# A hybrid block on one core: the inverse's levels on the full array, the scan's output products in one run, and a new instruction order

## The chip, the cores and the metric

The kernel runs on one core of one Trainium2 chip. The metric is the device time of one launch in microseconds (us). A core has a matrix engine (PE in the profile, TensorE here; its weight loads are listed apart as PEld), a vector engine (DVE), an activation engine (ACT), a general engine (POOL) and SP, which here only issues transfers. Each engine executes its instructions in the order in which they stand in the program, and engines wait for each other by semaphores. TensorE reads operands from the on-chip memory SBUF and writes results to PSUM, which has eight banks of 128 partitions x 512 float32.

## The reference, cut to what matters

32 sequences of 256 tokens with 128 features go through four residual stages:

```
x = x + attn_a(layernorm(x))      # gated delta rule
x = x + ffn(layernorm(x))         # silu(x Wg) * (x Wu), then Wd; hidden 384
x = x + attn_b(layernorm(x))      # convolution + state-space scan + gate
x = x + ffn(layernorm(x))
```

`attn_a` is a recurrence over tokens with a state S of 128 x 128 for each sequence:

```
S = S @ (a_t * (I - b_t * k_t k_t^T)) + b_t * v_t k_t^T ;  o_t = (q_t @ S) * g_t
```

Taken in chunks of 128 tokens, it becomes products of matrices and the inverse of a unit triangular 128 x 128 matrix for each chunk (the identity plus the decayed, beta-weighted products of keys). `attn_b` projects to z, x, B, C and dt, applies a causal convolution of four taps and silu to x, B and C, and computes for each of four heads `(C B^T * L) (x dt)` with `L[i, j] = exp(sum of dA from j+1 to i)`, adds a skip and what earlier tokens' state carries over, gates with silu(z), normalizes and projects. Everything is float32.

## The kernel before, in words

**Tiling.** Two sequences make a unit (`SEQS = 2`), so there are 16 units; a unit is NT = 4 tiles of 128 tokens, and most of its tiles are 128 partitions x 512 columns. A unit's work is four stages that follow one another: `attention` (stage 0, names ending in `_a`), `ffn` (stage 1, `_f`), `ssd` (stage 2, `_s`) and `ffn` again (stage 3, `_h`). Units don't depend on each other.

**Order.** No engine's order is the order of the source. `Planner` collects every operation of all 16 units with its engine, an assumed duration and an assumed latency, then `run` (L306) plays a list schedule: at each step it takes, over all engines, the operation that can start first, and among those of one engine that could start within 20 ns the one with the smallest key. The key (L316) is `at(unit)`, which is the unit's number times `period` (15,000 ns), plus how far from the end of its unit's longest chain the operation lies, plus an offset of its stage (`STAGE`). For the last three units `at` packs the starts closer (`LAST`). At most five units beside the oldest may be in work (`window`), a buffer must be free (`SLOTS`), a PSUM bank is given out only `EARLY` ns ahead of the work that fills it, and a change of ACT's function table counts as `SWITCH` ns in the key. The instructions are emitted in the order of the planned start times, and this is the program's order on each engine. Nothing in it adapts on the chip: an instruction whose operand is late holds what stands behind it on its engine.

**Helpers and lines.** All operations go through helpers, so the profile shows their lines: L214 `matmul`, L224 `transpose` (a product with the identity), L232 and L234 `act` (a copy, a function), L248 `vec`, L265 `pool`, L275 `dma` (issued by SP). A float32 product is executed as two passes, each with a weight load and a matmul record, so the counts in the profile are twice those of the source; a transpose is one pass. A form such as `128*64 128x64` is a pass whose weights take 128 rows and 64 columns of the array and that streams 64 columns.

**The inverse** (`attention`, L760 to L827). The 16 x 16 diagonal blocks of `diag` (the negated strictly triangular part of a chunk) go through DRAM: eight transfers write them to `blocks`, and eight more, one for each group of 16 partitions, broadcast them to `rows_n`. DVE inverts the blocks in 15 steps (`step`, `u`), and POOL spreads the result to the block diagonal of `x`. Then the blocks are doubled three times (`LEVELS = (16, 32, 64)`). A level transposes x (four passes), copies the result to SBUF (ACT, `t`), multiplies with `diag` (eight passes, `p1`), copies (ACT, `pm`), multiplies with x (eight passes, `p3`) and writes the off-diagonal blocks into x. Levels 16 and 32 stream all 128 columns of each tile, and DVE writes with a mask (COPY_PREDICATED, 128x512). Level 64 has a single off-diagonal block, and its operands are quarter tiles: 64 rows and 64 columns of the array, 64 columns streamed, three ACT copies of 64x256. In the profile p1 and p3 are `p_a<-t_a,neg_a` and `p_a<-x_a,pm_a`.

**The scan's output** (`ssd`, L1001 to L1024). For each sequence and each of its two tiles c, a product in bfloat16 makes the exponents (`pl`), ACT takes the exponential, DVE multiplies with the masked `cb` (`sm`), and then eight products (four heads, two halves of the tokens) write `sy_ps`. Each uses 128 rows and 64 columns of the array; the two halves stand beside each other in it. The eight products of a tile are operations of their own for the planner.

**The log-decay sums** (`ssd`, L928 to L936). `grid` holds 32 columns; a product with the triangle `le` sums them over tokens (`cs`). Its weights use 32 columns of the array.

What is touched beside this: the masks of the levels (L495 to L504, set up once) and the constants of the planner (L150 to L160).

Of the kernel before, what the change touches and what calls it, by code (L numbers as in the profile page):

```python
# [145 lines left out]
class Planner:  # L146
# [5 lines left out]
    SWITCH = 60000.0  # L152
    HOP, SLACK = 50.0, 0.0
    STAGE = (-100.0, -1400.0, -2700.0, -4400.0)
    EARLY = 2800.0
    SPARE = {"ps": 0.5, "m": 3, "l": 0.5, "t": 1, "s": 2, "d": 0.5, "g": 0.5, "b": 0.5, "e": 0.5}
    LAST = 0.26
    HALF = "be"
    RATE = 270.0
    LANES = 8  # L160
    SIZES = {"ps": 512, "m": 512, "l": 1024, "t": 64, "s": 32, "d": 512, "g": 8192, "b": 384, "e": 12288}
# [16 lines left out]

    def add(self, eng, busy, late, emit, outs, ins, table=None, after=(), lock=False):
# [4 lines left out]
        op.moves = 0.0  # L184
# [24 lines left out]
    def matmul(self, out, lhsT, rhs, start, stop, passes=2, cost=None):  # L209
# [10 lines left out]
        self.add("PE", busy, 165, emit, [out], [lhsT, rhs], after=after)  # L220

    def transpose(self, out, in_, ident, cost=109):
        def emit():
            self.tc.nc.tensor.transpose(real(out), real(in_), real(ident))  # L224

        self.add("PE", cost, 165, emit, [out], [in_, ident])
# [74 lines left out]
    def at(self, unit):  # L301

        late = max(0, unit - (self.units - 3))
        return (unit - late + late * self.LAST) * self.period

    def run(self):  # L306
# [20 lines left out]
        moved, landed = 0.0, []  # L327
        cands = {e: [] for e in engines}
# [6 lines left out]
        while len(order) < len(ops):  # L335
            best = None
            for e in engines:
                rest = []
                for op in cands[e]:
# [24 lines left out]
                if e == "ACT" and table is not None:  # L364
# [3 lines left out]
                    ]  # L368
                pick = min(same, key=lambda x: x[0])
# [4 lines left out]
            if op.eng == "ACT" and op.table and table not in op.table:  # L374
                t += 1300
                table = op.table[0]
                self.loads += 1
            for b in op.bufs:
# [49 lines left out]
def hybrid_block(ctx: ExitStack, tc: tile.TileContext, ins: dict, out: bass.AP):  # L428
# [35 lines left out]
    pl = Planner(tc, pools, period=15000.0, window=5)  # L464
# [31 lines left out]
    for d in LEVELS[:-1]:  # L496
        nb = P // (2 * d)
        m = pl.const([P, P], f"m_{d}")
        pool("memset", m, 0.0)
        v = m.rearrange("p (b h e) -> p b h e", h=2, e=d)[:, :, 1, :]  # L500
        pool("memset", v, 1.0)
        select(v, ALU.is_ge, 0, [[-2 * d, nb], [0, d]], 1)
        select(v, ALU.is_ge, d - 1, [[2 * d, nb], [0, d]], -1)
        mask_x.append(m.bitcast(I32)[:, None, :].to_broadcast([P, NT, P]))  # L504
# [20 lines left out]
    select(least, ALU.is_ge, 2 * (parts + 5), [[1, P]], -2)  # L525
    for i in range(2):
        sums_s.append(pl.const([P, NT, P], f"sums_s{i}", BF16, again=True))
# [120 lines left out]
    def attention(g, x):  # L648
# [120 lines left out]
        for b in range(NBLK):  # L769
            at = slice(b * BLOCK, (b + 1) * BLOCK)  # L770
            size = NT * BLOCK * BLOCK
            pl.dma(
                spread.part(at),
                blocks[0, b * size : (b + 1) * size].via(lambda ap: ap.partition_broadcast(BLOCK)),
                late=2100,
            )
# [19 lines left out]
        for lv, d in enumerate(LEVELS[:-1]):  # L796
            pt = bank([P, NT, P], f"pt_{n}_{d}")
            for j in range(NT):
                pl.transpose(pt[:, j, :], xi_f[:, j, :], ident)
            t = big([P, NT, P], f"t_{n}_{d}")  # L800
            copy(t, pt)
            p1 = bank([P, NT, P], f"p1_{n}_{d}")
            for j in range(NT):
                matmul(p1[:, j, :], diag[:, j, :], t[:, j, :], True, True)
            pm = big([P, NT, P], f"pm_{n}_{d}")
            copy(pm, p1)
            p3 = bank([P, NT, P], f"p3_{n}_{d}")
            for j in range(NT):
                matmul(p3[:, j, :], pm[:, j, :], xi_f[:, j, :], True, True)
            vec("copy_predicated", xi_f, mask_x[lv], p3, ins=(xi_f,), more=17)  # L810

        d = LEVELS[-1]
        lo, hi = slice(0, d), slice(d, P)
        pt = bank([P, NT, d], f"pt_{n}_{d}").part(lo)
        for j in range(NT):
# [293 lines left out]
```

## Time and profile before

| | us |
|---|---|
| median of 3 runs | 880.75 (879.32 to 882.31) |
| the profiled execution: device time | 885.61 |
| its span, from the first to the last instruction | 882.9 |
| TensorE busy (matmul records) | 842.9, 95% of the span |
| DVE / ACT / POOL busy | 687.5 / 608.1 / 351.9 |
| level-64 products and transposes (64*64 forms) | 12.9 + 11.2 + 6.6 |
| output products of the scan (128*64 form) | 41.9 |
| mean granted TensorE clock | 0.986 of full |

A row of a timeline is a run of equal instructions on one engine: its start, how long it lasts to the end of its last record, and their number. Matmul records overlap, since the ends of pipelined passes are modelled; what a run really takes from TensorE is the time from its start to the start of the next row. On TensorE with its work back to back the row of 128x128 passes advances by some 0.11 us a pass, and one of 512 streamed columns by some 0.43 us.

### The profile page before, as it was taken

What the parts mean: (1) busy time and instruction counts of PE and PEld (TensorE: products, weight loads), DVE (VectorE), ACT (ScalarE), POOL (GpSimd) and SP (SyncE); (2) the same over time, 40 slices, a digit from 0 to 9 for tenths busy, and PEclk for the clock granted to TensorE, in tenths of its full rate; (3) what the DMA queues carried; (4) which work ended last, traced back from release to release, by engine and by line L of the source; (5) the groups of instructions that cost most, each with busy time, mean ns of one, the idle gap of its engine ahead of it and who ended that gap; (6) DMA issues with size and microseconds to landing.
All of it is one profiled execution on the core that took longest, in us unless ns stands there. A gap on an engine that the chain in (4) does not pass through costs nothing.

```text
span 882.9 us, 16763 instructions
## 1 busy us (share of the span) xinstructions
PE 842.9 (95%) x5625; PEld 622.3 (70%) x5625; DVE 687.5 (78%) x2314; ACT 608.1 (69%) x1393; POOL 351.9 (40%) x559
## 2 busy tenths in 40 slices
PE   5879999999999999999999999999999999999798
PEld 3557776676858678685867868587675886765675
DVE  4695879877796878878887888877988467679963
ACT  5744477467685967677686767869477477579762
POOL 7974213151626335071633607155062231322550
PEclk9979999999999999999999999999999999999899
DMA  5211011000111101011110101111101000000001
GB/s 144 72 49 47 11 28 28 4 26 4 38 30 37 28 15 48 7 37 30 37 28 15 47 8 37 29 38 39 30 25 30 14 13 4 2 13 13 11 2 36
DMA packets 42149, 25.39 MB, mean 29 GB/s; under 512 B 18448, under 2 KB 37840, under 8 KB 42064
## 3 DMA queue, kind: packets, MB, share of 16 engines
q1 hardware_dynamic: 40768, 24.00, 10.2%
q8 instruction: 44, 0.72, 0.3%
q10 hardware_dynamic: 1296, 0.33, 0.2%
q14 instruction: 41, 0.34, 0.1%
HBM read 19.16 MB, written 5.14 MB: 28 GB/s over the span
## 4 chain that ended last, share of the span: by engine, by line
PE 67%; DVE 17%; ACT 10%; issue 2%; DMA 2%; POOL 1%; SPq 1%; DVEq 0%; POOLq 0%; ACTq 0%
PE p_a L214 8%; PE pc_s L214 5%; PE fu_h L214 5%; PE fg_h L214 5%; PE fy_f L214 4%; PE fu_f L214 4%; PE fg_f L214 4%; PE fy_h L214 3%; PE so_s L214 2%; DVE sm_s L248 2%; ACT L234 2%; PE kk_a L214 2%; PE wq_a L214 2%; DVE e_a L248 2%; PE sy_ps_s L214 2%
## 5 line engine op out<-in xcount | busy, mean ns | idle before, releaser
L248 DVE SCALAR_TENSOR_TENSOR cy_s<-pc_s,cw,cy_s 128x510 f32<-128x510 f32 (+2 forms) x192 | 137.0, 735 | 3.8 <-ACT cy_s L234 3.4
L234 ACT ACT_TABLE_LOAD x64 | 82.1, 1283 | 10.9 <-DMA bk<-in_L_attn_a_bk_dram 8.4
L214 PE MATMUL fy_f<-wdT,hT_f 128*128 128x128 f32 x384 | 75.7, 282 | 0.4 <-DVE hT_f L248 0.4
L214 PEld LDWEIGHTS fy_f<-wdT,hT_f 128*128 128x128 f32 x384 | 61.3, 191 | 15.7 <-issue 10.5
L214 PE MATMUL fy_h<-wdT,hT_h 128*128 128x128 f32 x384 | 71.7, 280 | 0.0
L214 PEld LDWEIGHTS fy_h<-wdT,hT_h 128*128 128x128 f32 x384 | 58.1, 191 | 10.2 <-issue 8.6
L214 PE MATMUL pc_s<-xT_s,w_xbc 128*128 128x512 f32 x128 | 62.3, 596 | 0.4 <-ACT zs_s L234 0.4
L265 POOL TENSOR_SCALAR ab_a<-ab_a 128x8 f32<-128x8 f32 x16 | 3.6, 227 | 147.1 <-ACT ab_a L234 147.0
L248 DVE TENSOR_TENSOR step_a<-rows_a,u_a 128x28 f32<-128x28 f32 (+14 forms) x240 | 53.3, 225 | 10.9 <-DMA rows_a<-blocks_a 5.6
L265 POOL TENSOR_TENSOR x_a<-u_a,blk 128x512 f32<-128x512 f32 x16 | 21.0, 1315 | 87.3 <-ACT qT_a L234 27.4
L234 ACT ACTIVATE cy_s<-pc_s,cb,cw 128x512 f32<-128x512 f32 x64 | 49.1, 780 | 8.3 <-PE pc_s L214 7.2
L248 DVE TENSOR_TENSOR u_a<-u_a,step_a 128x28 f32<-128x28 f32 (+14 forms) x240 | 50.2, 213 | 5.1
L214 PE MATMUL p_a<-x_a,pm_a 128*128 128x128 f32 (+1 forms) x384 | 52.7, 263 | 0.0
L214 PEld LDWEIGHTS p_a<-x_a,pm_a 128*128 128x128 f32 (+1 forms) x384 | 44.1, 173 | 11.9 <-issue 6.1
L234 ACT ACTIVATE fth_h<-fg_h 128x512 f32<-128x512 f32 x48 | 28.6, 597 | 34.3 <-PE fg_h L214 33.7
L214 PE MATMUL fu_f<-xT_f,wuT 128*128 128x512 f32 x96 | 49.8, 617 | 0.9 <-ACT fth_f L234 0.9
L214 PE MATMUL fu_h<-xT_h,wuT 128*128 128x512 f32 x96 | 50.1, 606 | 0.0
L214 PEld LDWEIGHTS p_a<-t_a,neg_a 128*128 128x128 f32 (+1 forms) x384 | 43.2, 178 | 9.7 <-ACT t_a L232 3.3
L214 PE MATMUL fg_h<-xT_h,wgT 128*128 128x512 f32 x96 | 49.2, 600 | 0.0
L214 PE MATMUL p_a<-t_a,neg_a 128*128 128x128 f32 (+1 forms) x384 | 48.5, 266 | 0.6 <-ACT t_a L232 0.5
L234 ACT ACTIVATE xn_s<-x,shift_s,rstd_s 128x128 f32<-128x128 f32 x64 | 26.4, 486 | 31.3 <-DVE shift_s L248 31.2
L265 POOL TENSOR_TENSOR xd_s<-xt_s,dt_s 128x512 f32<-128x512 f32 x32 | 32.8, 1043 | 37.1 <-ACT xt_s L232 37.1
(211 smaller groups left out, 2400.9 us busy)
## 6 DMA issues: line engine op xcount, KB each, us to landing
rows_a<-blocks_a SPq DMA_DIRECT2D x128, 64.0 KB
x<-in_L_attn_a_x_dram SPq DMA_DIRECT2D x16, 256.0 KB
dec_a<-row_a SPq DMA_DIRECT2D x16, 256.0 KB
out_dram<-x SPq DMA_DIRECT2D x16, 256.0 KB
blocks_a<-neg_a SPq DMA_DIRECT2D x128, 4.0 KB
cuts_s<-cut_s SPq DMA_DIRECT2D x48, 8.0 KB
sums_t<-cuts_s SPq DMA_DIRECT2D x32, 12.0 KB
sums_s<-cuts_s SPq DMA_DIRECT2D x16, 24.0 KB
```

The costliest lines, as they stand in the source:

```text
L214: self.tc.nc.tensor.matmul(real(out), lhsT=real(lhsT), rhs=real(rhs), start=start, stop=stop)
L234: self.tc.nc.scalar.activation(real(out), real(in_), func, bias=real(bias), scale=real(scale), **kw)
L248: getattr(self.tc.nc.vector, name)(real(out), *map(real, args), **{k: real(v) for k, v in kw.items()})
L265: getattr(self.tc.nc.gpsimd, name)(real(out), *map(real, args), **{k: real(v) for k, v in kw.items()})
```

## The change

Level 64 is written like the other two. In all three levels, `t` keeps the copied half of each pair of blocks in its second half and receives the first product in its first half, and the two products stream only the columns of the half that is needed (64 of 128 for each tile), with weights of 128 rows and 128 columns. The two ACT copies of a level and the masked DVE write take 256 columns in place of 512; level 64 has a masked DVE write where it had an ACT copy. The buffer `pm` is gone. The masks are set up with 64 columns, for three levels.

The eight `rows` transfers become one, which names the broadcast in its source. The 32 columns of `grid` become part of a 128-column constant tile that is otherwise zero (two of them, for even and odd units), so that the product uses 128 weight columns; only 32 rows of its result are read. The sixteen output products of a sequence are one batch: the first waits for all that any of them needs, and the planner puts nothing else on TensorE between them.

The planner also counts 150 ns (`CUT`) when TensorE changes between products of at most 64 weight columns and wider ones, and adds 2,000 ns (`KEEP`) to the key of an operation that would make it change. Its constants are others: `period` is 30,000, the stage offsets are (0, -8600, 1900, 0), `LAST` is 0.13, `EARLY` 1400, and `SHIFT` moves single units. With them the order on every engine is planned anew.

```diff
-    SWITCH = 60000.0
-    HOP, SLACK = 50.0, 0.0
-    STAGE = (-100.0, -1400.0, -2700.0, -4400.0)
-    EARLY = 2800.0
+    SWITCH = 64000.0
+    HOP, SLACK = 50.0, 30.0
+    STAGE = (0.0, -8600.0, 1900.0, 0.0)
+    EARLY = 1400.0
-    LAST = 0.26
+    LAST = 0.13
+    SHIFT = (0.0, -3200.0, 0.0, 0.0, 1500.0, 6600.0, 1600.0, 0.0, 0.0, 0.0, 0.0, 0.0, 0.0, 0.0, -7000.0, -5400.0)
+    CUT = 150.0
+    KEEP = 2000.0
+    def batch(self, ops):
+        for op in ops[1:]:
+            for p in op.preds.values():
+                if p not in ops and p.n not in ops[0].preds:
+                    ops[0].preds[p.n] = p
+                    p.succs.append(ops[0])
+        for op in ops:
+            op.batch = ops
...
+        op.cut = 0 if cols > P // 2 else 1
...
-        return (unit - late + late * self.LAST) * self.period
+        return (unit - late + late * self.LAST) * self.period + self.SHIFT[unit]
...
-                for op in cands[e]:
+                for op in cands[e] if e != "PE" or not rest_of else rest_of:
...
+                if e == "PE":
+                    same = [((k[0] + (self.KEEP if op.cut != cut else 0), k[1]), t, op) for k, t, op in same]
...
+            if op.eng == "PE":
+                t += self.CUT if op.cut != cut else 0.0
+                cut = op.cut
+                rest_of = [o for o in op.batch if not o.placed and o is not op]
...
-    pl = Planner(tc, pools, period=15000.0, window=5)
+    pl = Planner(tc, pools, period=30000.0, window=5)
...
-        for b in range(NBLK):
-            at = slice(b * BLOCK, (b + 1) * BLOCK)
-            size = NT * BLOCK * BLOCK
-            pl.dma(
-                spread.part(at),
-                blocks[0, b * size : (b + 1) * size].via(lambda ap: ap.partition_broadcast(BLOCK)),
-                late=2100,
-            )
+        pl.dma(
+            spread,
+            blocks.via(
+                lambda ap: ap[0, :].rearrange("(b n) -> b n", b=NBLK)[:, None, :].to_broadcast(
+                    [NBLK, BLOCK, NT * BLOCK * BLOCK]
+                )
+            ),
+            late=2100,
+        )
...
-        for lv, d in enumerate(LEVELS[:-1]):
+        for lv, d in enumerate(LEVELS):
+            nb = P // (2 * d)
+            halves = xi_f.rearrange("p t (b h e) -> p t b h e", h=2, e=d)
             pt = bank([P, NT, P], f"pt_{n}_{d}")
             for j in range(NT):
                 pl.transpose(pt[:, j, :], xi_f[:, j, :], ident)
             t = big([P, NT, P], f"t_{n}_{d}")
-            copy(t, pt)
-            p1 = bank([P, NT, P], f"p1_{n}_{d}")
+            t_halves = t.rearrange("p t (b h e) -> p t b h e", h=2, e=d)
+            copy(t_halves[:, :, :, 1, :], pt.rearrange("p t (b h e) -> p t b h e", h=2, e=d)[:, :, :, 0, :])
+            p1 = bank([P, NT, nb, d], f"p1_{n}_{d}")
             for j in range(NT):
-                matmul(p1[:, j, :], diag[:, j, :], t[:, j, :], True, True)
-            pm = big([P, NT, P], f"pm_{n}_{d}")
-            copy(pm, p1)
-            p3 = bank([P, NT, P], f"p3_{n}_{d}")
+                matmul(p1[:, j, :, :], diag[:, j, :], t_halves[:, j, :, 1, :], True, True)
+            copy(t_halves[:, :, :, 0, :], p1)
+            p3 = bank([P, NT, nb, d], f"p3_{n}_{d}")
             for j in range(NT):
-                matmul(p3[:, j, :], pm[:, j, :], xi_f[:, j, :], True, True)
-            vec("copy_predicated", xi_f, mask_x[lv], p3, ins=(xi_f,), more=17)
-        d = LEVELS[-1]
...
+                matmul(p3[:, j, :, :], t[:, j, :], halves[:, j, :, 1, :], True, True)
+            vec("copy_predicated", halves[:, :, :, 1, :], mask_x[lv], p3, ins=(xi_f,), more=17)
...
-        grid = small_([P, 2, NH, NT], f"grid_{n}")
+        few = slice(0, 2 * NH * NT)
+        grid = grids[g % 2][:, few].rearrange("p (o h j) -> p o h j", o=2, h=NH)
...
-        pc = bank([P, P], f"cs_{n}").part(few)
-        matmul(pc, grid.rearrange("p o h j -> p (o h j)"), le, True, True)
+        pc = bank([P, P], f"cs_{n}")
+        matmul(pc, grids[g % 2], le, True, True)
+        pc = pc.part(few)
...
+            ms = []
             for c in range(2):
...
-                for h in range(NH):
-                    for to in (slice(0, P // 2), slice(P // 2, P)):
-                        matmul(
-                            py[:, c, h * HD : (h + 1) * HD].part(to), m[:, h, to], xd[:, c, h, :], True, True,
-                        )
+                ms.append(m)
+            pl.batch([
+                matmul(
+                    py[:, c, h * HD : (h + 1) * HD].part(to), m[:, h, to], xd[:, c, h, :], True, True, cost=62,
+                )
+                for c, m in enumerate(ms) for h in range(NH) for to in (slice(0, P // 2), slice(P // 2, P))
+            ])
```

## The prediction

> **What bounds the kernel now.** I read the page first (busy shares, the slices), then TensorE's busy time by stretches, then TensorE's timeline row by row, then the waits. TensorE is the bound: it is the one engine that is nearly always busy, and ahead of slice 5 and around slice 38 it is not.
>
> ```profile
> PE 842.9 (95%) x5625; PEld 622.3 (70%) x5625; DVE 687.5 (78%) x2314; ACT 608.1 (69%) x1393; POOL 351.9 (40%) x559
> ...
> PE   5879999999999999999999999999999999999798
> ...
> PEclk9979999999999999999999999999999999999899
> ```
>
> The stretches (columns: start:end, length, busy us and number of records of TensorE, its weight loads, DVE, ACT and POOL, granted clock, DMA share and GB/s):
>
> ```profile
> 0.00:44.00 44.00, 30.44 (x139) 20.58 (x140) 25.24 (x106) 28.19 (x85) 37.75 (x85) 1.00 0.42 107
> 44.00:100.00 56.00, 48.76 (x291) 38.40 (x290) 43.09 (x155) 26.16 (x66) 28.23 (x41) 0.91 0.16 42
> 100.00:820.00 720.00, 709.69 (x4813) 524.82 (x4813) 578.10 (x1946) 517.82 (x1161) 261.94 (x400) 1.00 0.09 24
> 820.00:850.00 30.00, 25.18 (x243) 18.74 (x239) 26.25 (x69) 22.36 (x51) 18.50 (x27) 0.89 0.03 6
> 850.00:882.90 32.90, 28.79 (x152) 19.74 (x150) 14.80 (x41) 13.53 (x30) 5.53 (x10) 0.97 0.08 25
> ```
>
> In the long middle TensorE idles 10.3 us of 720. Start and tail idle 13.6 + 7.2 + 4.8 + 4.1 = 29.7 us, and in two of them the granted clock is down (0.91, 0.89), which costs about 0.09 x 56 + 0.11 x 30 = 8 us more. So an edit is worth what it changes of TensorE's own occupancy, plus what the new order makes of about 40 us of idle time and 8 us of clock. ACT (69%) and DVE (78%) get lighter for nothing unless TensorE waits for them.
>
> **Occupancy.** A pass's price is the start of the next row less its own start. Level 64 and the narrow products sit between wide ones (TensorE's timeline):
>
> ```profile
> 400.94 1.05 PE L214 MATMUL p_a<-t_a,neg_a 128*128 128x128 f32 x8
> 401.83 0.59 PE L214 MATMUL fg_f<-xT_f,wgT 128*128 128x512 f32 x1
> ...
> 417.38 0.38 PE L214 MATMUL fy_f<-wdT,hT_f 128*128 128x128 f32 x2
> 417.69 0.68 PE L214 MATMUL p_a<-t_a,neg_a 64*64 64x64 f32 x8
> 418.30 1.12 PE L214 MATMUL fu_h<-xT_h,wuT 128*128 128x512 f32 x2
> ```
>
> Eight full passes take 401.83 - 400.94 = 0.89 us, 0.11 each. Two `fy_f` passes ahead of the quarter tiles take 0.31, not 0.22: 0.09 us to enter. The eight quarter passes take 0.61. Over all start times in the trace the medians are: full pass 112 ns, transpose 109; quarter pass 58, quarter transpose 56, entering +93, leaving +90. There are 59 runs of quarter tiles, mostly four to a unit.
>
> ```profile
> 385.14 0.38 PE L214 MATMUL po_a<-pr_a,k_a 128*128 128x128 f32 x2
> 385.46 0.34 PE L214 MATMUL sy_ps_s<-xd_s,sm_s 128*64 128x64 f32 x4
> 385.72 0.49 PE L214 MATMUL po_a<-pr_a,k_a 128*128 128x128 f32 x2
> 386.14 1.03 PE L214 MATMUL sy_ps_s<-xd_s,sm_s 128*64 128x64 f32 x28
> ```
>
> The output products: two `po_a` passes take 0.32 (0.09 to enter), four narrow passes 0.26: 4 x 0.032 (the median over pairs) and 0.12 to leave. So a run costs 0.21 us beside its work. There are 50 such runs. `cs` (128*32) takes 133 ns a pass, 93 to enter and 69 to leave, once a unit.
>
> **What will a pass of 128 weight columns cost that streams 64?** No such row exists; the nearest is `pe`, with 128 weight columns and 8 streamed:
>
> ```profile
> 381.63 0.38 PE L214 MATMUL fy_h<-wdT,hT_h 128*128 128x128 f32 x2
> 381.85 0.29 PE L214 MATMUL pe_s<-dA_s,le 128*128 128x8 f32 x2
> 382.00 0.47 PE L214 MATMUL fy_h<-wdT,hT_h 128*128 128x128 f32 x2
> 382.36 0.41 PE L224 MATMUL pt_a<-ident,x_a 128*128 128x128 f32 x2
> ```
>
> Six passes take 0.73 us, as six full ones do (0.67) and a little more, though two of them stream almost nothing. What `pe` seems to save (0.15 to the next row) `fy_h` gives back (0.36 for two): the weight loads keep their step of 0.11. Two sections of the Trainium skill, page "TensorE: Matmul & The Clock Gate", part here. "Back-to-back issue gap" prices a matmul by its streamed columns alone, so half the columns would be about half the time; "LDWEIGHTS" prices a load by weight columns, 128 / 1.2 = 107 ns. By the first, taking the 58 ns of the quarter row, levels 16 and 32 (32 product passes a unit) would save 32 x 54 ns = 1.73 us, and level 64 would lose its transposes only; by the second nothing is saved and level 64 pays full passes. The row decides for the second: 112 ns. The ends are 58 and 112.
>
> **The sum on TensorE, 16 units.**
> - Level 64 on full weights: 16 passes x (112 - 58) + 4 transposes x (109 - 56) = 1.08 us a unit: +17.2.
> - Its 59 mode runs gone: 59 x 0.183 = -10.8.
> - Output products: at most two runs a unit, so 50 to 32: 18 x 0.213 = -3.8.
> - `cs` padded: 2 x (112 - 133) - 93 - 69 = -0.20 us a unit: -3.3.
> Together -0.7 us. At 58 ns a pass it would be another 16 x (1.73 + 0.86) = -41.
>
> **What other engines get.** An ACT copy of 128x512 takes 594 and 583 ns, one of 64x256 takes 364 to 367; a copy of 4x128 takes 249 and one of 128x128 287, so columns set it, and I take 0.365 for 128x256: 4 x 0.22 + 0.365 (the last copy moves to DVE) = -1.25 us a unit, 20 of 608. The masked write is 728 ns for 512 columns; the nearest half-sized DVE reads of PSUM take 413 to 421: 2 x -0.31 + 0.41 = -0.2 us a unit. Both lie behind TensorE's work for other units: 0. Without that cover a unit's inverse chain would be 1.5 us shorter in levels 16 and 32 and 1.1 longer in level 64, still near nothing. Masks and the zeroed grids change a few POOL memsets ahead of the first unit's inverse: 0. The second grid is free again two units later: 0. The batch makes a sequence's first eight output products wait for the second tile's exponential and mask (0.59 + 0.68 us); behind them on TensorE stand other units' products, which the plan puts ahead instead: 0, or 16 x 2 x 1.3 = 41 us if nothing stood ready.
>
> **The row transfer.** Seven of eight issues go, 0.46 us apart on SP. In place of them comes a wait: the one transfer needs all eight block writes, where the first row transfer could leave at once.
>
> ```profile
> 344.73 4.22 SPq L275 DMA_DIRECT2D blocks_a<-neg_a  x7
> 349.00 3.66 SPq L275 DMA_DIRECT2D rows_a<-blocks_a  x8
> ```
>
> Before: 3.7 us of issues and 2.15 until the last landed (the chain shows it at 88.30), 5.8 us. After: some 1.8 (SP's longest wait for `cuts`, a like pair), 0.4 to issue, 2.15, and the spread of 128 rows of 4 KB at about 0.24 us: 7 more on each of 16 engines, 1.7. Sum 6.1. Here a rule speaks against the change: "DMA: Bandwidth & Descriptors", section "Why a DMA increments its semaphore by 16 and not by 1", has a transfer use the largest number of engines up to 16 that divides the slowest dimension of both sides; the source's is now 8. Then 15 more rows on each of 8 engines: 3.6, sum 8.0. Loss +0.3 to +2.2 us a unit. Behind SP's wait stand input loads and sums for other units, whose consumers come later. DVE waited 5.6 us in all for these rows; TensorE has other units' work: 0, but up to 2 at the first unit.
>
> **The order.** This decides. Of the 40 us idle, some 14 stay (TensorE starts at 10.3 us, behind the first loads; 4 us lie behind its last pass). Of the other 26, plus 8 of clock, I take two fifths: -14. Doubling `period` lets older units finish first; the last three units' starts are now packed to 386.9, 390 and 392.4 us of key, which mixes their tails, where all three now wait for DVE's convolution around 820 to 832. Bounds: -30 (nearly all of it) to +26 (below).
>
> Span 882.9 - 0.7 - 14 = 868. The profiled execution took 885.61, 4.9 above the median; from span to median it is -2.15, so **866 us**.
>
> **The rivals.**
> - *Half the streamed columns is half the time.* -41 on TensorE, of which DVE and hand-offs would return a part (I take 40%): 866 - 25 = 841. The row of `pe` speaks against it. 5%.
> - *The edits cancel and the order is worth nothing.* The middle is at 98.6% already, and the start hangs on loads and POOL (37.75 busy of 44). 880, from 877 to 884. 12%.
> - *Slower: the inverse's hand-offs come uncovered.* A level hands over three times between TensorE and ACT or DVE, nine times a unit. Each is a copy (0.37) and TensorE's resumption (waits for ACT ahead of weight loads show 0.2 to 0.7), say 0.8 us. Today rows of `fy_f`, `fu_h` and `pvq` from other units stand between them. With keys 30 us apart, units are mixed less, and an in-order queue waits. Two bare hand-offs a unit are 16 x 2 x 0.8 = 26 us; with head and tail unimproved the kernel becomes slower from the first quarter of one on (0.25 x 0.8 x 16 = 3). Against it: the plan places other work wherever it expects a wait. About 893, from 884. 25%.
> - *The forecast*: 850 to 877, 58%.
>
> **Range and chances.** From 848 (7% below) to 893 (half of the slower case above, 13%). A difference of 0.3%, 2.6 us, is about what can be told. Faster: the forecast, the 5%, a quarter of the second rival: 0.66. Same 0.09, slower 0.25.
>
> **What would show it.** `p_a` rows of 128x64 that advance by 0.11 us a pass (0.06 would prove the first rival); no 64*64 and no 128*32 forms; `sy_ps` in 16 to 32 runs; ACT busy near 588; TensorE idle in the first 100 and last 63 us down from 29.7 to about 20. I am wrong if TensorE's waits for `t` or `p_a` in the middle grow beyond 10.3 us, or if start and tail stay as they are.

## The result, and the profile after

The changed kernel takes 935.45 us (934.11 to 936.46), beside 880.37 us of the kernel before in the same comparison: 1.0622 times as long, with a 95% interval of 1.0598 to 1.0647. The forecast was 866 us and its range ended at 893. The profiled execution took 934.78 us and its span is 933.1 us, 50.2 more than before.

From the page of the changed kernel (busy us and share of the span, the slices, the granted clock, and the chain that ended last by engine and by line):

```profile
PE 845.4 (91%) x5625; PEld 636.9 (68%) x5625; DVE 677.2 (73%) x2330; ACT 608.2 (65%) x1391; POOL 353.0 (38%) x562
...
PE   5588998999998899999999899898997898998788
...
PEclk9889999999999899999999999999998999989999
...
PE 50%; DVE 19%; ACT 12%; DMA 11%; POOL 3%; issue 2%; SPq 2%; ACTq 0%; DVEq 0%; POOLq 0%
DMA rows_a<-blocks_a 9%; PE p_a L227 5%; DVE cy_s L264 4%; PE fg_h L227 4%; PE fy_f L227 4%; PE fu_h L227 4%; ACT L250 3%; PE fy_h L227 3%; PE fg_f L227 3%; PE fu_f L227 3%; PE pz_s L227 2%; SPq L291 2%; PE pc_s L227 2%; PE so_s L227 2%; DVE x L264 2%
```

TensorE executes the same 5,625 passes and is busy for about as long. Its row of slices, solid before from slice 4 to 37, now has eights and a seven throughout. At the head of the chain's list stands a transfer, `rows_a<-blocks_a`, with 9% of the span: the one that replaced eight.

The same stretches as before (start:end, length, busy us and records of TensorE, weight loads, DVE, ACT and POOL, granted clock, DMA share, GB/s):

```profile
0.00:44.00 44.00, 24.13 (x106) 16.13 (x106) 25.46 (x91) 21.20 (x62) 39.74 (x86) 0.94 0.39 100
44.00:100.00 56.00, 49.00 (x284) 38.13 (x285) 40.67 (x168) 29.48 (x83) 26.77 (x43) 0.90 0.20 48
100.00:820.00 720.00, 675.82 (x4610) 516.99 (x4609) 534.17 (x1845) 480.69 (x1082) 251.58 (x381) 0.98 0.09 24
820.00:850.00 30.00, 25.84 (x94) 15.33 (x95) 17.89 (x61) 20.21 (x47) 4.40 (x9) 0.88 0.00 0
850.00:933.10 83.10, 70.57 (x535) 50.35 (x533) 58.99 (x168) 56.64 (x119) 30.54 (x44) 0.98 0.06 17
```

In the middle TensorE idles 720 - 675.82 = 44.2 us, where it idled 10.3, and the clock there is 0.98 where it was 1.00. By 820 us the changed kernel has done 5,000 passes (106 + 284 + 4610); before it had done 5,243. The edits' own price is not the reason. TensorE's timeline (start, length, count of a run):

```profile
343.12 1.06 PE L227 MATMUL p_a<-t_a,neg_a 128*128 128x64 f32 x8
344.01 0.61 PE L240 MATMUL pt_a<-ident,x_a 128*128 128x128 f32 x4
...
449.80 2.09 PE L227 MATMUL sy_ps_s<-xd_s,sm_s 128*64 128x64 f32 x64
451.81 0.38 PE L227 MATMUL fy_f<-wdT,hT_f 128*128 128x128 f32 x1
```

Eight passes of 128 weight columns and 64 streamed ones take 344.01 - 343.12 = 0.89 us, 0.11 each: the streamed half buys nothing, as forecast. The output products of two sequences have met in one run: 64 passes in 2.01 us, one change of tile form where there were several.

To see where the 50 us went I took, over the whole trace, the step from each pass's start to the next start, and split it: the form's usual step, what is added where the tile form changes, and the rest (waits, and passes at a lower clock). The split is rough: the second column takes in waits that happen to fall on a change of form. At the prices in the prediction the 20 narrow runs that are left would be some 4 us.

| us | usual steps | form changes | the rest |
|---|---|---|---|
| before | 769.4 | 30.6 | 68 |
| after | 785.0 | 11.5 | 122.5 |

The edits cost 15.6 and return 19.1; the other 54.5 us are waits and clock.

**One transfer, followed to TensorE.** DVE's two longest waits (total us, times, longest), and the second of them in the kernel before:

```profile
DVE hT_h L264 <- PE fu_h L227: 38.2, 30, 4.6
DVE step_a L264 <- DMA rows_a<-blocks_a: 35.4, 14, 6.6
```

```profile
DVE step_a L248 <- DMA rows_a<-blocks_a: 5.6, 6, 1.7
```

The first (12.9 us before) stays at 37.7 in the first experiment below, where only the transfer is put right, so it is not the transfer's.

And the timeline of all engines around one of the sixteen transfers (in brackets the idle time ahead, and what ended it):

```profile
384.03 0.63 SPq L291 DMA_DIRECT2D rows_a<-blocks_a  x1
...
387.06 0.69 DVE L264 TENSOR_TENSOR hT_f<-fth_f,fu_f 128x512 f32<-128x512 f32 x1 [0.17 <-PE fu_f L227]
...
390.08 0.44 PE L227 MATMUL fy_f<-wdT,hT_f 128*128 128x128 f32 x2
...
390.84 0.22 DVE L264 TENSOR_TENSOR step_a<-rows_a,u_a 128x60 f32<-128x60 f32 x1 [3.08 <-DMA rows_a<-blocks_a]
...
391.48 0.15 DVE L264 TENSOR_TENSOR f_s<-dt_s,pl_s 128x4 f32<-128x4 f32 x1
...
391.77 1.22 POOL L281 TENSOR_TENSOR xe_s<-xt_s,f_s 128x256 f32<-128x256 f32 x2 [3.11 <-DVE f_s L264]
...
392.44 0.70 PE L227 MATMUL pf_s<-xe_s,cb_s 128*128 128x256 f32 x2 [1.92 <-POOL xe_s L281]
```

The rows arrive 6.8 us after SP began to issue their transfer. The plan had counted `late` (2,100 ns) and 524,288 bytes at `RATE` (270 bytes a ns, 1,942 ns): 4.04 us. (For the eight, with the same `late`, its sum is 7 x 0.45 + 2.1 + 0.24 = 5.5 us, and in the kernel before the first step followed 5.5 to 6.5 us after the first issue where DVE waited for it: there the plan was nearly right.) So the first inversion step stands in DVE's order some 2.7 us too early, and DVE stops for 3.1 us. Behind it is not only the inverse. `f_s` belongs to another unit's scan; POOL's `xe_s` waits for it, and TensorE's `pf_s` for that. TensorE has nothing else ahead of it in its order, and idles 1.92 us.

That is not all that it loses. The stretches around this gap (same columns as above):

```profile
388.00:390.50 2.50, 2.50 (x22) 2.29 (x20) 0.00 (x0) 2.49 (x5) 0.67 (x1) 1.00 0.27 70
390.50:392.40 1.90, 0.02 (x1) 0.00 (x0) 1.50 (x7) 0.47 (x2) 0.62 (x2) 1.00 0.00 0
392.40:394.00 1.60, 1.56 (x8) 1.40 (x8) 1.60 (x3) 0.00 (x0) 0.59 (x1) 0.84 0.00 0
394.00:396.00 2.00, 2.00 (x34) 1.78 (x33) 1.30 (x6) 0.00 (x0) 0.00 (x0) 0.50 0.00 0
396.00:398.00 2.00, 2.00 (x40) 1.64 (x38) 1.53 (x3) 0.00 (x0) 0.73 (x1) 0.77 0.00 0
398.00:400.00 2.00, 2.00 (x20) 1.91 (x17) 1.84 (x4) 0.30 (x2) 0.73 (x1) 1.00 0.03 8
```

One microsecond after TensorE has resumed, its granted clock falls to half for about 3.4 us: 0.16 x 1.6 + 0.50 x 2 + 0.23 x 2 = 1.7 us more, for a gap of 1.9.

### The profile page after: what moved, and what is told of

The parts are those of the page before. It is cut to its first block, busy times and chain, and to the rows that moved or that the text cites. A ratio compares the mean times of both kernels' runs of the same rounds, so it can differ in the third digit from the quotient of the medians.

```text
span 933.1 us, 16686 instructions
## 1 busy us (share of the span) xinstructions
PE 845.4 (91%) x5625; PEld 636.9 (68%) x5625; DVE 677.2 (73%) x2330; ACT 608.2 (65%) x1391; POOL 353.0 (38%) x562
## 4 chain that ended last, share of the span: by engine, by line
PE 50%; DVE 19%; ACT 12%; DMA 11%; POOL 3%; issue 2%; SPq 2%; ACTq 0%; DVEq 0%; POOLq 0%
DMA rows_a<-blocks_a 9%; PE p_a L227 5%; DVE cy_s L264 4%; PE fg_h L227 4%; PE fy_f L227 4%; PE fu_h L227 4%; ACT L250 3%; PE fy_h L227 3%; PE fg_f L227 3%; PE fu_f L227 3%; PE pz_s L227 2%; SPq L291 2%; PE pc_s L227 2%; PE so_s L227 2%; DVE x L264 2%
## 5 line engine op out<-in xcount | busy, mean ns | idle before, releaser
L264 DVE TENSOR_TENSOR step_a<-rows_a,u_a 128x60 f32<-128x60 f32 (+14 forms) x240 | 53.4, 226 | 39.0 <-DMA rows_a<-blocks_a 35.4
L227 PEld LDWEIGHTS fy_h<-wdT,hT_h 128*128 128x128 f32 x384 | 61.3, 191 | 21.6 <-issue 19.4
L264 DVE TENSOR_TENSOR hT_h<-fth_h,fu_h 128x512 f32<-128x512 f32 x48 | 32.9, 684 | 39.7 <-PE fu_h L227 38.2
L227 PEld LDWEIGHTS p_a<-x_a,t_a 128*128 128x128 f32 x384 | 52.3, 192 | 5.7 <-ACT t_a L248 3.0
L227 PE MATMUL p_a<-t_a,neg_a 128*128 128x64 f32 x384 | 55.4, 268 | 0.7 <-ACT t_a L248 0.6
L227 PE MATMUL p_a<-x_a,t_a 128*128 128x64 f32 x384 | 55.0, 264 | 0.5 <-ACT t_a L248 0.4
L227 PEld LDWEIGHTS p_a<-t_a,neg_a 128*128 128x128 f32 x384 | 52.0, 195 | 4.3 <-ACT t_a L248 3.2
L264 DVE TENSOR_TENSOR u_a<-u_a,step_a 128x60 f32<-128x60 f32 (+14 forms) x240 | 51.8, 219 | 3.8
L264 DVE TENSOR_TENSOR hT_f<-fth_f,fu_f 128x512 f32<-128x512 f32 x48 | 32.6, 683 | 29.6 <-PE fu_f L227 23.6
L281 POOL TENSOR_TENSOR sy_s<-xt_s,d_skip 128x512 f32<-128x512 f32 x32 | 33.0, 1043 | 54.1 <-ACT xt_s L248 54.1
L227 PE MATMUL fg_f<-xT_f,wgT 128*128 128x512 f32 x96 | 50.0, 639 | 1.8 <-ACT xT_f L248 0.9
```

Source lines behind the costliest of these rows:

```text
L227: self.tc.nc.tensor.matmul(real(out), lhsT=real(lhsT), rhs=real(rhs), start=start, stop=stop)
L264: getattr(self.tc.nc.vector, name)(real(out), *map(real, args), **{k: real(v) for k, v in kw.items()})
L281: getattr(self.tc.nc.gpsimd, name)(real(out), *map(real, args), **{k: real(v) for k, v in kw.items()})
```

## The experiments

Two theories. **The landing** (T in the expectations): the row transfer comes later than the plan assumes, and DVE, held by it, starves other units. **The constants** (O, then C): the new `period`, `SHIFT`, `STAGE` and the others make a worse order, wherever the rows land. A third, that the rival of the prediction was right (the inverse's hand-offs uncovered), would show as TensorE's waits for `t_a` and `x_a`. Where an experiment is planned anew, its order changes everywhere; where it says that the order is kept, every engine's order is that of its parent but for the transfers' issues. Each ratio is to the kernel before, run beside it; 0.01 is 8.8 us. Intervals are 95%.

### The landing, with the order kept

`after_eight`: the changed kernel, with the eight old transfers issued at the place of the one.

```diff
-            engine.dma_start(out=real(out), in_=real(in_))
+            for o, i in as_ or [(out, in_)]:
+                engine.dma_start(out=real(o), in_=real(i))
...
+            as_=[
+                (
+                    spread.part(slice(b * BLOCK, (b + 1) * BLOCK)),
+                    blocks[0, b * size : (b + 1) * size].via(lambda ap: ap.partition_broadcast(BLOCK)),
+                )
+                for b in range(NBLK)
+            ],
```

> The changed kernel with every engine's order left exactly as it is, but eight row transfers issued at the place of the one. T (the one row transfer lands some 2.7 us later than the plan has DVE start on it; DVE, in order, stands still and what waits for DVE stands still with it): DVE's wait for rows falls from 35.4 us to under 8, and the time from 935 to about 900 (some 2.2 us earlier, 14 times). O (the new order is worse by itself, its hand-offs bare, and the wait for rows is one symptom among many): 925 or more.

904.29 us, ratio 1.0228 (1.0196 to 1.0260), against 1.0622: 0.0394, or 34.7 us, come back. Its page and DVE's wait for the rows:

```profile
PE 829.5 (92%) x5625; PEld 627.8 (70%) x5625; DVE 675.9 (75%) x2330; ACT 606.9 (68%) x1391; POOL 353.3 (39%) x562
```

```profile
DVE step_a L264 <- DMA rows_a<-blocks_a: 4.2, 6, 1.2
```

The wait falls from 35.4 to 4.2 us, and the span by 933.1 - 898.1 = 35.0. TensorE's order is the same in both kernels, so its busy time can be compared: 845.4 - 829.5 = 15.9 us of the 35.0 are the same passes taking longer, and 19.1 are idle time. The granted clock accounts for the 15.9: stretches at half clock cost 30.9 us within the span of the changed kernel and 12.7 here, 18.2 less, a part of them over idle time. This also explains the page of after: a "busy" TensorE of 845.4 us holds 16 us that come of half speed.

`before_one`: the kernel before, its order kept, with one transfer issued at the place of the last of the eight.

```diff
+            o, i = out, in_
+            if all_:
+                all_[0] -= 1
+                if all_[0]:
+                    return
+                o, i = all_[1:]
-            engine.dma_start(out=real(out), in_=real(in_))
+            engine.dma_start(out=real(o), in_=real(i))
...
+        once = [NBLK, spread, blocks.via(
+            lambda ap: ap[0, :].rearrange("(b n) -> b n", b=NBLK)[:, None, :].to_broadcast(
+                [NBLK, BLOCK, NT * BLOCK * BLOCK]
+            )
+        )]
...
-                late=2100,
+                late=2100, all_=once,
```

> The kernel before with every engine's order left as it is, but the one row transfer issued at the place of the last of the eight. T: DVE waits some 2 us more a unit for rows, 25 to 40 us in all, and the time rises from 880 to 900 to 915. O: 880 to 886, the wait is covered.

897.41 us, ratio 1.0152 (1.0117 to 1.0187): the transfer alone makes the old kernel 13.4 us slower, a little less than the landing theory expected. DVE's waits:

```profile
DVE step_a L248 <- DMA rows_a<-blocks_a: 34.5, 12, 4.8
```

Almost the wait that the changed kernel has (35.4), for well under half the loss. 28.9 us of added wait become 13.4 us here, and the granted clock stays at 0.986. In the changed kernel 31.2 us of wait (35.4 - 4.2) become 19.1 us of idle TensorE, and 15.9 us of clock come on top. So the price of a late transfer depends on what TensorE has in hand, and on whether its gaps grow long enough for the clock to fall.

`after_late`: the changed kernel, planned anew with a latency that the transfer keeps.

```diff
-            late=2100,
+            late=4800,
```

> The changed kernel with the one row transfer planned to land 2.7 us later (late 4800 in place of 2100), and so planned anew. T: DVE's wait for rows under 8 us, time 875 to 895. O: 915 or more.

908.38 us, ratio 1.0275 (1.0240 to 1.0309), between the two ranges that were expected. DVE waits 3.0 us for the rows. The one transfer is harmless once the plan knows when it lands, and yet the kernel is 24 us slower than before.

### The constants

`before_consts`: the kernel before with the new `SWITCH`, `SLACK`, `STAGE`, `EARLY`, `LAST`, `SHIFT` and `period`, and none of the edits.

```diff
...
-    STAGE = (-100.0, -1400.0, -2700.0, -4400.0)
-    EARLY = 2800.0
+    STAGE = (0.0, -8600.0, 1900.0, 0.0)
+    EARLY = 1400.0
...
-    pl = Planner(tc, pools, period=15000.0, window=5)
+    pl = Planner(tc, pools, period=30000.0, window=5)
```

> The kernel before with the new planning constants alone (SWITCH, SLACK, STAGE, EARLY, LAST, SHIFT, period): eight row transfers, quarter tiles, no batch, no count of mode changes. T: 870 to 890. O: 910 or more, with TensorE idle in the middle as in the changed kernel.

946.32 us, ratio 1.0720 (1.0674 to 1.0766): the constants alone cost the old kernel 63 us, with no late transfer (its wait for rows is 5.6 us, as before).

`eight_old`: `after_eight` with the old constants (`SHIFT` all zero).

```diff
-    SWITCH = 64000.0
-    HOP, SLACK = 50.0, 30.0
-    STAGE = (0.0, -8600.0, 1900.0, 0.0)
-    EARLY = 1400.0
+    SWITCH = 60000.0
+    HOP, SLACK = 50.0, 0.0
+    STAGE = (-100.0, -1400.0, -2700.0, -4400.0)
+    EARLY = 2800.0
-    LAST = 0.13
-    SHIFT = (0.0, -3200.0, 0.0, 0.0, 1500.0, 6600.0, 1600.0, 0.0, 0.0, 0.0, 0.0, 0.0, 0.0, 0.0, -7000.0, -5400.0)
+    LAST = 0.26
+    SHIFT = (0.0,) * 16
...
-    pl = Planner(tc, pools, period=30000.0, window=5)
+    pl = Planner(tc, pools, period=15000.0, window=5)
```

> The changed kernel with eight row transfers at the place of the one, planned with the old constants (SWITCH, SLACK, STAGE, EARLY, LAST, period; SHIFT zero), still with the count of mode changes and the batch. C (of the 20 us that stay after the row transfer, the new constants cost all): 872 to 887. L (the full-array level 64 costs its 17 us without return): 897 or more.

873.52 us, ratio 0.9894 (0.9855 to 0.9932): 29 us better than `after_eight`, and faster than before, although here DVE waits 20.0 us for rows that land later than planned.

`one_old`: all edits with one transfer, the same old constants, and the landing told to the plan (against the changed kernel, the diff above and this).

```diff
-            late=2100,
+            late=4800,
```

> The changed kernel, one row transfer and full-array level 64 included, with the old constants and the row transfer planned to land 2.7 us later. T (the transfer costs by standing in the plan too early, not by its own length): DVE waits under 8 us for rows, 868 to 880, as with eight transfers (873.5). If its own length or its wait on SP costs: 885 or more.

864.54 us, ratio 0.9799 (0.9765 to 0.9833): faster than both kernels. Its page:

```profile
PE 818.9 (95%) x5625; PEld 624.9 (73%) x5625; DVE 672.9 (78%) x2330; ACT 591.4 (69%) x1381; POOL 347.9 (40%) x562
```

The gain of 18 us on the kernel before belongs to the edits as a set (full-array levels, one transfer, the padded `cs`, the batch, `CUT` and `KEEP`), in an order planned for them; of these only the transfer and level 64 were tried alone. Split as above, its TensorE has 784.9 us of usual steps, 6.5 of form changes and 57.8 of the rest.

`old_2100`: `one_old` with `late` 2100 again, planned anew: the fourth corner.

```diff
-            late=4800,
+            late=2100,
```

> The changed kernel, all its edits, with the old constants, and the one row transfer planned as in the change (late 2100). It closes the square of constants and landing (changed kernel 935, landing put right 908, constants put right and landing too 864.5). T: DVE waits 25 to 40 us for rows, 880 to 900. If the wait is covered in this order: 862 to 872.

899.06 us, ratio 1.0181 (1.0134 to 1.0228). DVE's waits:

```profile
DVE step_a L264 <- DMA rows_a<-blocks_a: 55.1, 14, 8.7
```

The four corners, as ratios to before:

| | new constants | old constants |
|---|---|---|
| rows planned at 2100 | 1.0622 | 1.0181 |
| rows planned at 4800 | 1.0275 | 0.9799 |

The wrong landing costs 0.035 and 0.038 (31 and 34 us), the constants 0.044 and 0.048 (39 and 42 us). The two add up, as closely as orders planned anew can be compared (below). But DVE's wait is not itself the price: 50.6 us more of it (55.1 less 4.5) cost 34 us here.

### Which constant

Each of these is `one_old` with some of the new constants put back; the rows land as planned in all of them (DVE waits between 1.5 and 8.2 us).

`old_stage` and `old_early`:

```diff
-    STAGE = (-100.0, -1400.0, -2700.0, -4400.0)
+    STAGE = (0.0, -8600.0, 1900.0, 0.0)
```

```diff
-    EARLY = 2800.0
+    EARLY = 1400.0
```

> The run at 864.5 (all edits, landing put right, old constants) with the new stage offsets alone (0, -8600, 1900, 0 in place of -100, -1400, -2700, -4400). G (the offsets cost: they put the state-space stage and the last feed-forward behind the first feed-forward of younger units): 890 or more of the 908 that all new constants gave. Otherwise: 856 to 874.

> The run at 864.5 with EARLY at 1400 alone (PSUM banks given out later ahead of what fills them). E (TensorE waits because products are planned later): 880 or more. Otherwise: 856 to 874.

`old_stage` takes 874.88 us, ratio 0.9905 (0.9882 to 0.9927): 9 us of loss. `old_early` takes 862.03 us, ratio 0.9764 (0.9737 to 0.9791): no loss. It is the fastest of all that were run; from `one_old` it can't be told apart, since the intervals overlap.

`old_shift`:

```diff
-    LAST = 0.26
-    SHIFT = (0.0,) * 16
+    LAST = 0.13
+    SHIFT = (0.0, -3200.0, 0.0, 0.0, 1500.0, 6600.0, 1600.0, 0.0, 0.0, 0.0, 0.0, 0.0, 0.0, 0.0, -7000.0, -5400.0)
...
-    pl = Planner(tc, pools, period=15000.0, window=5)
+    pl = Planner(tc, pools, period=30000.0, window=5)
```

> The run at 864.5 with the period doubled and the new LAST and SHIFT, which are counted in it. F (the unit starts cost, above all in the tail): 880 or more, TensorE's idle time behind 700 us up. Otherwise: 856 to 874.

907.38 us, ratio 1.0276 (1.0238 to 1.0313): 42 us, the whole loss of the constants. It was then taken apart: `only_period` has the lines of `period` and `LAST` from this diff, `only_shift` that of `SHIFT`.

> The run at 864.5 with the period doubled (30000, LAST 0.13, so that the last units' spacing stays 3.9 us) and no SHIFT. The run with period, LAST and SHIFT together took 907. P (the doubled period costs): 890 or more. If SHIFT alone costs: 872 or less.

> The run at 864.5 with SHIFT alone, period 15000 and LAST 0.26. If the shifts of single units cost by themselves: 890 or more, units unevenly spaced in the middle. P: 872 or less.

`only_period` takes 893.44 us, ratio 1.0120 (1.0097 to 1.0144): 28 us. `only_shift` takes 873.64 us, ratio 0.9892 (0.9872 to 0.9913): 8 us. The same 600 us of the middle, first of `one_old`, then of `only_period`, then of `old_shift`:

```profile
100.00:700.00 600.00, 591.39 (x4187) 459.33 (x4188) 482.07 (x1704) 424.11 (x988) 228.34 (x355) 1.00 0.11 28
```

```profile
100.00:700.00 600.00, 582.36 (x4056) 443.13 (x4055) 485.78 (x1643) 424.77 (x979) 233.13 (x354) 1.00 0.10 27
```

```profile
100.00:700.00 600.00, 572.34 (x3886) 433.61 (x3885) 465.78 (x1650) 401.95 (x942) 225.10 (x345) 0.99 0.11 27
```

TensorE's idle time grows from 8.6 to 17.6 and 27.7 us, and 131 and 301 fewer passes are done in the same time. Passes differ in length; each priced by its form's usual step, the work that is not yet done at 700 us is 20 and 35 us more than in `one_old`: most of the loss of 28 and 42 is there ahead of the tail that `LAST` packs.

Two runs went the other way, from `after_eight`: `eight_period` sets `period` back to 15000, `eight_switch` doubles `SWITCH` to 128000, to have fewer changes of ACT's function table.

```diff
-    pl = Planner(tc, pools, period=30000.0, window=5)
+    pl = Planner(tc, pools, period=15000.0, window=5)
```

```diff
-    SWITCH = 64000.0
+    SWITCH = 128000.0
```

> As the changed kernel with eight row transfers at the place of the one (904), but the period back at 15000; the other new constants stay. P (the doubled period, which mixes units less, is what costs): 870 to 888. S (the stage offsets, shifts and the rest cost): 897 or more.

> As the same kernel (904), with SWITCH at 128000, so that it has the ratio to the period that it had before. If the 14 more table loads on ACT (78 against 64, 1.28 us each) are what costs: loads fall to under 70 and the time to 880 to 892. If they are only what a worse order shows: 898 or more.

901.16 us, ratio 1.0212 (1.0182 to 1.0242), and 909.39 us, ratio 1.0307 (1.0271 to 1.0343). Neither recovers anything. With the other new constants in place, setting the period back brings nothing, though with the old ones doubling it costs 28 us (`LAST` stays at 0.13 in `eight_period`, so the starts of the last units also move from 3.9 to 2 us apart); so the constants' loss is shown for the set and not for one of them. Nor is it the table loads: `eight_period` has 66 of them and `old_shift` 60, the fewest, beside 78 in the changed kernel and 68 in `one_old`. `eight_switch` still has 76, so it tested less than it was meant to.

### Level 64, and how much a new order moves by itself

`old_quarter` is `eight_old` with level 64 on quarter tiles, as before the change, counted as a tile form of its own; `quarter_planned` is that with the eight transfers planned as eight, in the old loop over `NBLK`.

```diff
-        op.cut = 0 if cols > P // 2 else 1
+        op.cut = 0 if cols > P // 2 else 2 if lhsT.lanes[1] - lhsT.lanes[0] <= P // 2 else 1
...
-        for lv, d in enumerate(LEVELS):
+        for lv, d in enumerate(LEVELS[:-1]):
...
+        p1 = bank([P, NT, d], f"p1_{n}_{d}").part(hi)
+        for j in range(NT):
+            matmul(p1[:, j, :], diag[:, j, hi].part(lo), t[:, j, :], True, True)
```

> As the run with old constants and eight row transfers, but level 64 on quarter tiles as before; quarter tiles count as a mode of their own. C: TensorE's sum says quarter tiles take 17.2 less and 48 to 59 mode runs more (8.8 to 10.8), so 6 to 8 us faster than that run, as far as it shows. L: 15 or more faster.

> As the run with old constants and level 64 on quarter tiles (869), but with the eight row transfers planned as eight, each with its own landing, in place of one that the plan lets land 1.7 us early. T: DVE's wait for rows falls from 19.4 us to under 8, and the time to 855 to 866. Rival (in this order the wait is covered): 867 to 873.

869.41 us, ratio 0.9850 (0.9820 to 0.9880), and 874.56 us, ratio 0.9896 (0.9857 to 0.9935). The first is 4 us faster than `eight_old` with its full-array level. The second should have gained from rows that land as planned (DVE waits 7.2 us in place of 19.4), and lost 4 us, outside both ranges that were expected. Both differences are no larger than what a mere change of order does, which two controls show: `HOP`, the planner's price for a hand-over, 60 in place of 50, in the kernel before (`before_hop`) and in `after_eight` (`eight_hop`, where `SLACK` stays 30.0).

```diff
-    HOP, SLACK = 50.0, 0.0
+    HOP, SLACK = 60.0, 0.0
```

> A control: the kernel before with one planning constant moved that describes nothing of the change (the assumed hand-off HOP, 50 to 60 ns), so that every order is planned anew. It says how far a new order alone moves the time. Both theories take this to be under 10 us: 874 to 894. If it is 20 or more, a difference of 20 us between two planned orders names no cause.

> The same control on the changed kernel with eight row transfers at the place of the one and its new constants (904 us): HOP 50 to 60 ns, planned anew. Both theories: 894 to 914. More than that, and its 20 us over the kernel before may be this one order and not the constants.

889.29 us, ratio 1.0076 (1.0051 to 1.0101), and 902.48 us, ratio 1.0227 (1.0193 to 1.0262): 6.7 us and nothing. In `eight_hop` DVE even waits 15.1 us for the rows, 10.9 more than in `after_eight`, and the time is the same: a wait of DVE is not a price by itself. So between kernels that were planned anew I take a difference under some 10 us to name no cause, though two trials are few. That holds for level 64, for `STAGE` and for `SHIFT` alone; it does not hold for the pairs with the order kept.

## Why the prediction was wrong

- **"The row transfer": the time of the transfer was right.** It said 6.1 to 8.0 us from the last block write to the last row, 8.0 if the rule of the Trainium skill held that a transfer uses the largest number of engines up to 16 that divides the slowest dimension of both sides ("DMA: Bandwidth & Descriptors", "Why a DMA increments its semaphore by 16 and not by 1"). In 13 of the sixteen units SP waits 1.1 to 1.4 us for the block writes (at most 3.1), and where DVE waited for the rows its first step follows 6.3 to 7.0 us after that: 7.9 in the median. While one such transfer ran, the DMA engines' share (last but one number) was 0.46, 7.4 of 16 engines:

```profile
305.20:309.70 4.50, 4.50 (x29) 3.52 (x28) 1.38 (x2) 1.44 (x3) 0.00 (x0) 1.00 0.46 117
```

- **"The row transfer": the step that failed is its last, "DVE waited 5.6 us in all for these rows; TensorE has other units' work: 0, but up to 2 at the first unit."** In its place, 34.7 us. It asked whether TensorE has other work while the unit waits, and looked for what is queued behind the wait on SP. What is queued behind it on DVE is what matters: DVE makes other units' operands, in an order fixed by a plan that counted on 4.04 us. Both numbers were at hand: a latency of 4.3 to 6.2 us from the issue by my own sum, 4.04 by the planner's two constants, so up to 2.2 us late in each of sixteen units, 35 us at most. DVE waited 35.4 us, but in fourteen units and for rows that were some 2.7 us late; that the two figures agree so well is luck. And the step from DVE's wait to the time could not have been had from them: about the same wait cost 34.7 us in one order and 13.4 in another.
- **The clock had no price in it.** Of the 34.7 us nearly half (15.9) is TensorE's work taking longer, at half speed around its gaps. The sum counted 8 us of lost clock as something to win and never as something that a new wait costs.
- **"The order", -14 us: the sign failed.** In its place, the constants cost 39 to 42 us with the edits and 63 without. With the landing put right (`after_eight`), TensorE idles 33.9 us before 100 and behind 820 us, where it was to fall from 29.7, and 34.7 us in the middle, where it had idled 10.3; of the lost clock nothing came back (12.7 us within the span, 12.8 before). I took two fifths of the idle time at start and tail as a gain and bounded the loss by the hand-offs (+26). The middle, at 98.6%, was treated as something that the order could not spoil. The page of before could not have told me what the new order would be; it could have told me that nearly all the risk lay on the side of loss, since 10 of 720 us were left to win and everything to lose.
- **The slower rival** named loss in the right direction, 893 us, but not the place. In `after_late`, 24 us slower than before, TensorE's weight loads wait 4.1 us for `t_a` and 1.2 for `x_a`; before they waited 3.3 for `t_a`, 1.5 for `pm_a` and 0.7 for `x_a`. So the inverse's hand-offs are no barer there. In the changed kernel they wait 6.1 and 12.0 us, and 6.1 and 5.4 in `after_eight`, whose order is the same: the rest is the late rows again.
- **"The sum on TensorE", -0.7 us: right in kind, and better than said.** (In brackets what the sum had.) The usual steps rose by 15.6 us (16.5 by the sum: 17.2 for level 64, less 0.7 for `cs`). Form changes fell by 19.1 in the changed kernel and by 24.1 in `one_old` (17.2 by the sum): the mis-sized term is the output products, of which 19 or 20 runs are left where I assumed 32: 2.6 us more. What is still over in `one_old`, some 4 us, I put down to waits that fell on changes of form. Passes with 64 streamed columns cost 112 ns, and the first rival falls. The two sections of the Trainium skill, "TensorE: Matmul & The Clock Gate", do not part as the prediction has it: "Back-to-back issue gap" gives its formula by streamed columns for an isolated matmul alone, and says that in a stream of weight loads and matmuls both set the spacing; the 112 ns here agree with that.
- **"What other engines get"** held in its durations: the copies and the masked write of 256 columns, by form (busy us, mean ns, idle before):

```profile
L248 ACT COPY t_a<-p_a 128x256 f32<-128x256 f32 x48 | 17.9, 372 | 27.8 <-PE p_a L227 27.4
...
L264 DVE COPY_PREDICATED x_a<-m,p_a 128x256 f32<-128x256 int32 x48 | 20.7, 431 | 12.0 <-PE p_a L227 9.7 <-POOL x L281 2.2
```

372 for 365 and 431 for 410 ns. ACT's busy time didn't fall to 588 but stayed at 608.2, because the new order loads a function table 78 times in place of 64, 14 x 1.283 = 18 us.
- **The forecast's 866 us** is about what the edits give under the old constants with the landing told to the plan, 864.5, but that is luck in good part. The split has -8.6 us on TensorE's steps and form changes where the sum said -0.7, and about -10 on the rest where it said -14. And the -14 was to come from less idle time at start and tail and a better clock: in `one_old` TensorE idles 42.1 us in all (861.0 - 818.9), where it idled 40.0 before; only some 4 us of clock came back (8.5 us lost within the span, 12.8 before).

What stays open: why the set of new constants makes so much worse an order. The runs place most of the loss ahead of the tail, and exclude the landing and the table loads. That keys 30 us apart mix the units less and leave TensorE with less to choose from fits `only_period`, but `eight_period` speaks against it as the whole reason. `SWITCH` and `SLACK` were not tried alone with the old constants, nor were the batch, `CUT` and `KEEP`, or the padded `cs` without the rest, nor a single transfer that reaches all sixteen DMA engines.

## What to carry to other kernels

In a program whose order is fixed ahead, a transfer's latency is not only its consumer's matter: compare when it really lands with when the order expects it, and price the difference at everything that stands behind the consumer on its engine, for every repetition. Merging transfers saves issues but moves the landing, so the plan's latency has to be measured again; here that one number is worth 31 to 34 us, and the merged transfer 13 in the old order. And judge an edit and the constants of a scheduler apart, with the order kept where that can be done, since a new order alone moved this kernel by 7 us in one trial and by nothing in another, and a bad set of constants by 63.

## What the runs showed of the hardware

**A short gap on TensorE is often paid twice.** The changed kernel has 23 gaps over 1 us on TensorE past 20 us, 49.1 us in all. Of the 11 of 1.9 us or more, 10 had the clock at half within 3 us of their end (in one it had fallen before the gap); of the 12 shorter ones, 2. Over all twenty traces it was 68 of 82, and 43 of 130 of the shorter. The clock stays at half for about 3.4 us, or a multiple of it, and each 3.4 us of half clock lose 1.7 us. The changed kernel has 13 half-clock stretches, which cost 30.9 us within its span, where the kernel before has 6 and 12.8, `after_eight` 6 and 12.7, and `one_old` 2 and 8.5. (Some of it falls on idle time, where it costs nothing.) So I would count a wait of 2 us that reaches TensorE as 3 to 4, an estimate from these counts. The Trainium skill ("TensorE: Matmul & The Clock Gate", "What's actually happening") has the clock fall after an idle window of about 3.4 us; here gaps of 1.9 us were mostly enough, and the measurement decides.

**One transfer for eight is slower than eight.** Where DVE waited for the rows, its first step came 5.5 to 6.5 us after the first issue of the eight (median 5.8, in the kernel before), with seven further issues on the way; with the one it came 6.3 to 7.0 us after (median 6.7). While one ran, the DMA engines' share was 0.46, about half of them. That one transfer on all sixteen would be faster was not run.
